# The last image's gate taken from sums of numerators, its last product in two halves, its flag earlier, its last store on ScalarE

## The chip, the cores and the metric

One core of a Trainium2 chip runs the kernel. The metric is the device time of one execution in microseconds; the kernel before has a median of 2622.44 us over three runs. Engines are named as the profile names them: PE is TensorE (PEld its weight loads), DVE is VectorE, ACT is ScalarE, POOL is GpSimd, SP is SyncE; a q behind a name is the engine's sequencer. Times without a unit's origin count from the start of the profiled span.

## What is computed

A batch of 16 images of 256 channels, 28 x 28, passes through a residual block whose two convolutions are lookups: each channel's 3 x 3 patch is softly assigned to 16 centroids, and the assignment weights mix a table.

```python
def amm_conv3x3(x, centroids, w_sub, stride=1):
    patches = jax.lax.conv_general_dilated_patches(x, (3, 3), (stride, stride), 'SAME')
    ...
    d = jnp.sum(p * p, axis=-1)[..., None] - 2.0 * jnp.einsum('bncs,cks->bnck', p, centroids) + ...
    attn = jax.nn.softmax(-d, axis=-1)
    lut = jnp.einsum('cks,cso->cko', centroids, w_sub)
    out = jnp.einsum('bnck,cko->bno', attn, lut)
def se_layer(x, w1, b1, w2, b2):
    s = jnp.mean(x, axis=(2, 3))
    s = jax.nn.relu(s @ w1 + b1)
    s = jax.nn.sigmoid(s @ w2 + b2)
    return x * s[:, :, None, None]
out = amm_conv3x3(x, centroids1, wsub1); out = jax.nn.relu(bn_inference(out, ...))
out = amm_conv3x3(out, centroids2, wsub2); out = bn_inference(out, ...)
out = se_layer(out, se_w1, se_b1, se_w2, se_b2)
return jax.nn.relu(out + x)          # x here: group-normed; the block's input is added once more outside
```

What matters here is the end: the gate `s` of an image needs the mean of all 784 positions of the second convolution, after its batch norm, before a single output value can be written.

## The kernel before

Per layer and image there are four blocks: two halves of the input channels times two halves of the 28 rows (392 positions, `N`). A block makes logits (line 418), exponentials, numerators (`na`, `nb`, lines 469 and 483) and a reciprocal, and ends with nine scaled numerator tiles `q` of 128 x 392 (`qp` in pairs of 784 columns, `qo` single). Eight products a image and layer then combine the `q` of four blocks with weights by Strassen's scheme (Winograd's form): seven multiplications of 128-channel halves, numbered 5 to 12 after their place in the schedule (6 and 7 are one, cut in two). A product is nine matmuls of 128 x 128 by 128 x 392, fp32, each of which leaves two records in the profile. POOL forms the differences of `q` in place (`mix`, lines 560 and 562); VectorE, ScalarE and POOL combine the products' results into four regions: c11, c12 (output half 0, row halves 0 and 1), c21, c22 (output half 1).

The order of work is written out by hand: `at(cl, sub, f, ...)` files a job under a place, all jobs are sorted by place and issued in that order, and each engine takes its own instructions in that order. For the last image of layer 2 (`n == 2 * B - 1`, b = 15), `g` is its first place, products 9 to 12 stand at `g + 9` to `g + 12`, and no later block fills TensorE. PSUM is four tiles of two banks each (`ps0` to `ps3`); a tile is given by a turning rule (`ROLES`, `EARLY`) or by a fixed `tag`, and a new user of a tile waits until the last reader of the old one is done.

End of an image in layer 2: batch norm with a running sum (`norm_out`, line 608, or `norm_both`, line 617), `se_hidden` (lines 839 to 851, a matmul over the means and two small activations), `se_gate` (853 to 862, a matmul and exponentials), `se_recip` (865), and the finish. For images 0 to 14 the finish is spread over ScalarE and POOL while later blocks run: `finish_gate` (869), `finish_norm` (877, group norm of x into `xn`), `finish_sum` (883), `finish_relu` (888), `finish_add` (891), `store` (902). For image 15 it is `finish_fast`: two VectorE passes a half, lines 896 and 899, and the store by SP. Product 12 enters c21 by line 592, which is the last thing that the mean waits for.

Numerator sums have a second use: `wsum` collects the sums of every block, and `flags` (lines 911 to 922) checks them for overflow; `flag_sum` (924) adds the flags over partitions with a matmul and casts the sum to an integer. Every engine loads that integer (line 1170), and where it is positive a slow fallback runs (line 1172 on); here it is skipped by a branch.

## Time and profile before

| | |
|---|---|
| median of 3 runs | 2622.44 us (2621.93 to 2623.15) |
| profiled execution | 2621.02 us |
| its span | 2619.5 us |
| PE busy | 2583.4 us (99%) |
| DVE, ACT, POOL busy | 1761.6, 1360.3, 1900.5 us |
| granted TensorE clock, mean | 0.998 |

The span is one execution as the hardware profiler saw it; the time of a run has some 1.5 us more around it. A timeline row gives start, duration, engine, line, operation, tiles and, in brackets, the idle time before it and who ended it. A matmul's recorded duration is longer than its share of a stream, since matmuls overlap: a product's pace is read from starts or from the chain of waits. ACTIVATION_READ_ACCUMULATOR rows belong to the activation with a running sum before them.

### The profile page before, as it was taken

Reading aid. Unit: us, or ns where it says so; the run is one execution under the profiler, and the core shown is the slowest. Engines: PE = TensorE matmul, PEld = TensorE weight load, DVE = VectorE, ACT = ScalarE, POOL = GpSimd, SP = SyncE. Lnnn points to the kernel's source line nnn. Section 1 sums busy time; section 2 is a strip of 40 time slices with the busy share of each in tenths; the row PEclk is TensorE's granted clock in tenths of the full one; section 3 lists DMA queues with packets and bytes.
Section 4 is the critical chain, followed back from the end, with each engine's and each line's share of the span. In section 5 each row is a group of like instructions: output and inputs, shape, how many; then the busy total and the mean of one; then the engine's idle time right before and its main releaser. Section 6 shows DMA issues by size and latency. Waiting matters only on the chain.

```text
span 2619.5 us, 85666 instructions
## 1 busy us (share of the span) xinstructions
PE 2583.4 (99%) x36984; PEld 1265.0 (48%) x36984; DVE 1761.6 (67%) x3759; ACT 1360.3 (52%) x1879; POOL 1900.5 (73%) x1316
## 2 busy tenths in 40 slices
PE   6999999999999999999999999999999999999997
PEld 2444454444444444444444444444444444444444
DVE  5776656666566665566676767766776767677665
ACT  5444544444444454444445555555555556555553
POOL 3786666766568766677666887878878778878786
PEclk9999999999999999999999999999999999999999
DMA  8556656655555566554664444444444443444441
GB/s 223 157 162 180 196 152 188 169 170 173 155 144 148 168 184 178 166 166 135 179 168 103 112 109 129 119 122 119 103 118 128 126 117 104 117 123 121 117 121 45
DMA packets 217959, 374.37 MB, mean 143 GB/s; under 512 B 29752, under 2 KB 188520, under 8 KB 217576
## 3 DMA queue, kind: packets, MB, share of 16 engines
q1 hardware_dynamic: 211256, 335.24, 48.1%
q0 software_dynamic: 6320, 33.58, 3.6%
q8 instruction: 295, 4.83, 0.8%
q14 instruction: 88, 0.72, 0.1%
HBM read 288.93 MB, written 79.80 MB: 141 GB/s over the span
## 4 chain that ended last, share of the span: by engine, by line
PE 97%; DMA 1%; DVE 1%; POOL 0%; ACT 0%; SPq 0%; issue 0%; DVEq 0%; POOLq 0%; ACTq 0%
PE acc L553 52%; PE lg L418 17%; PE na L469 14%; PE nb L483 14%; DMA wall<-home 0%; DMA pt<-home 0%; PE sep L855 0%; DVE r L511 0%; SPq L404 0%; ACT e L429 0%; POOL qp L562 0%; PE sep L844 0%; DMA home<-xpad 0%; DMA xt<-in_x 0%; DVE rb L526 0%
## 5 line engine op out<-in xcount | busy, mean ns | idle before, releaser
L553 PE MATMUL acc<-qp,wall 128*128 128x392 f32 x3072 | 1096.8, 500 | 0.9 <-DVE qp L545 0.7
L429 ACT ACTIVATE e<-lg 128x784 f32<-128x784 f32 x960 | 737.9, 820 | 635.1 <-PE lg L418 632.2
L562 POOL TENSOR_TENSOR qp<-qp,qp 128x784 f32<-128x784 f32 x512 | 943.5, 1867 | 155.6 <-DVE qp L545 155.1
L553 PEld LDWEIGHTS acc<-qp,wall 128*128 128x128 f32 x3072 | 566.4, 190 | 507.1 <-issue 56.9
L526 DVE STREAM_SHUFFLE rb<-r 128x392 f32<-128x392 f32 x1024 | 551.0, 604 | 0.0
L418 PE MATMUL lg<-pt,wd 32*32 32x392 f32 x16256 | 483.2, 502 | 7.2 <-DMA wall<-home 4.9
L497 DVE SCALAR_TENSOR_TENSOR r<-nb,kst,r 128x392 f32<-128x392 f32 x128 | 80.1, 626 | 458.6 <-ACT r L493 444.1
L545 DVE TENSOR_TENSOR qp<-na,rb 128x784 f32<-128x784 f32 x352 | 333.8, 972 | 59.4 <-PE na L469 48.2
L483 PE MATMUL nb<-e,cwb 64*32 64x392 f32 x8192 | 373.6, 492 | 0.1
L469 PE MATMUL na<-e,cwa 64*32 64x392 f32 x8192 | 373.7, 492 | 0.0
L534 POOL TENSOR_TENSOR qo<-qo,rb 128x392 f32<-128x392 f32 x128 | 132.5, 1035 | 310.2 <-DVE rb L522 309.4
L511 DVE RECIPROCAL r<-r 128x392 f32<-128x392 f32 x128 | 333.2, 2603 | 4.4
L534 POOL TENSOR_TENSOR qp<-qp,rb 128x784 f32<-128x784 f32 x160 | 295.8, 1858 | 3.2 <-ACT hpad L604 0.4
L483 PEld LDWEIGHTS nb<-e,cwb 64*32 64x32 f32 x8192 | 189.5, 107 | 176.6 <-issue 20.8
L469 PEld LDWEIGHTS na<-e,cwa 64*32 64x32 f32 x8192 | 182.2, 106 | 182.4 <-issue 72.9
L418 PEld LDWEIGHTS lg<-pt,wd 32*32 32x32 f32 x16256 | 120.9, 103 | 281.8 <-issue 243.1
L553 PE MATMUL acc<-qp,w_A 128*128 128x392 f32 x512 | 182.7, 499 | 0.0
L493 ACT ACTIVATE r<-nb,kst 128x392 f32<-128x392 f32 x128 | 86.7, 678 | 162.3 <-PE nb L483 162.3
L453 POOL TENSOR_TENSOR z<-z,mx 128x1568 f32<-128x1568 f32 x32 | 91.8, 2869 | 94.8 <-DVE mx L447 94.8
L553 PE MATMUL acc<-qo,wall 128*128 128x392 f32 x384 | 157.8, 493 | 0.0
L539 ACT COPY qp<-na 128x784 f32<-128x784 f32 x160 | 130.0, 812 | 26.2 <-PE na L469 24.4
L553 PEld LDWEIGHTS acc<-qp,w_A 128*128 128x128 f32 x512 | 94.7, 190 | 82.1 <-DVE qp L545 19.8
(159 smaller groups left out, 1642.8 us busy)
## 6 DMA issues: line engine op xcount, KB each, us to landing
pt<-home SPq DMA_DIRECT2D x762, 209.0 KB
pt<-home SPq DMA_DIRECT2D x762, 104.5 KB
home<-xpad SPq DMA_DIRECT2D x30, 899.0 KB
xt<-in_x SPq DMA_DIRECT2D x30, 784.0 KB
out_dram<-y SPq DMA_DIRECT2D x32, 392.0 KB
d_wS<-st SPq DMA_DIRECT2D x12, 192.0 KB
wall<-d_wS SPq DMA_DIRECT2D x4, 576.0 KB
wall<-in_ws SPq DMA_DIRECT2D x3, 576.0 KB
```

The source lines that it names most:

```text
L418: nc.tensor.matmul(bk[32 * c : 32 * c + 32, :N].rearrange("p (r w) -> p r w", w=W), lhsT=wts["wd", u["hh"]][32 * i : 32 * i + 32, mm, c, : ...
L429: nc.scalar.activation(eg[:, 2 * i : 2 * i + 2, :], bk[:, :, :N], AF.Exp, scale=2.0)
L453: nc.gpsimd.tensor_tensor(zk, zk, mx.unsqueeze(2).to_broadcast([P, N // 4, K]), ALU.subtract)
L469: nc.tensor.matmul(bs[32 * i : 32 * i + 32, r, :N], lhsT=wts["cwa", u["hh"]][64 * r : 64 * r + 64, mm, i, :], rhs=es[64 * r : 64 * r + 64, ...
L483: nc.tensor.matmul(bs[32 * i : 32 * i + 32, r, :N], lhsT=wts["cwb", u["hh"]][64 * r : 64 * r + 64, mm, i, :], rhs=es[64 * r : 64 * r + 64, ...
L511: nc.vector.reciprocal(u["r"], u["r"])
L526: nc.vector.stream_shuffle(rb[:, r, :], u["r"], mask_of(2 * mm + r))
L534: nc.gpsimd.tensor_tensor(q, q, u.pop(("rb", mm)), ALU.mult)
L539: nc.scalar.copy(pair(u, mm), u.pop(("na", mm))[:, :, :N])
L545: nc.vector.tensor_mul(pair(u, mm), u.pop(("na", mm))[:, :, :N], rb)
L553: nc.tensor.matmul(accs[key][:, :N], lhsT=wl[w][:, k, :], rhs=us["q", k], start=first and n == 0, stop=last and n == len(ks) - 1,)
L562: nc.gpsimd.tensor_tensor(pair(out_u, mm), pair(in0, mm), pair(in1, mm), ALU.subtract)
```

## The change

- **Sums instead of products for the gate** (image 15). The mean of product 11's and product 12's results over positions is the weight matrix times the sum of the `q` over positions. ScalarE sums each of the nine `q` of block 0 (`total_act`, an activation with running sum whose output is thrown away), VectorE those of block 3 (`total_dve`); POOL takes their difference, since product 12 uses block 0 minus block 3 (`total_sub`). ScalarE multiplies the nine 128 x 128 weight blocks of A12 and of A22 by these sums, one activation a block (`weigh`), VectorE adds the nine (`weigh_sum`), and two one-column matmuls against ones add over partitions (`rest_sum`). `norm_ahead` norms c11 and c21 before those products are in, with their running sums; `se_hidden` adds the two missing means as further terms.
- **Product 11** is issued in three parts (5, 2 and 2 matmuls): rest_sum's matmuls stand between the first two, se_hidden and the flag's matmul between the last two, and se_gate's matmul before product 12. **Product 12** is issued as two halves of 196 columns in PSUM tiles 2 and 3 (`open_last`). Its result is no longer added to c21 and normed; `finish_ahead` folds gate, norm and x for the 392 positions beforehand, and `finish_last` takes each half from PSUM with two passes of 196 columns. c11, c12 and c22 are finished (`norm_join`, `finish_part`) ahead of them.
- **The flag**: `flags` moves behind rest_sum, `flag_sum` into product 11.
- **Stores**: image 15 has four instead of two: 784, 392 and 196 columns by SP, the last 196 by ScalarE.
- **Image 14** is finished by two activations into PSUM tile 3 (`gate_wide`) and two VectorE passes each (`finish_wide`) instead of by ScalarE and POOL; its norm of x moves ahead, to before product 9.
- **Image 15's x** is loaded into a patch buffer instead of an exponential's, at `g + 7` instead of `g + 11`, and normed at `g + 8`; products 9, 10 and 11 get PSUM tiles 0, 1 and 0. POOL's subtraction for the first pair at `g + 10` comes just before the others.

The diff, cut to its core:

```diff
+    def spare_of(n0, n, i=0):
+        return pts[i].rearrange("p s n -> p (s n)")[:, n0 : n0 + n]
...
+    def product(key, us, w, ks, first=True, last=True, step=None, cols=(0, N), tag=None):
+        if first and key not in accs:
+            accs[key] = bank("acc", step, step and ROLES["acc"][step % 2], EARLY["acc"].get(step) if tag is None else tag)
         for n, k in enumerate(ks):
             nc.tensor.matmul(
-                accs[key][:, :N], lhsT=wl[w][:, k, :], rhs=us["q", k],
+                accs[key][:, : cols[1] - cols[0]], lhsT=wl[w][:, k, :], rhs=us["q", k][:, cols[0] : cols[1]],
...
+        terms = [(k, ysum[:, k, i : i + 1]) for k in range(NB) for i in range(2 if b >= B - 1 else 1)]
+        if (b, "rest") in ys:
+            terms += [(k, ys[b, "rest"][:, k : k + 1]) for k in range(NB)]
+        for n, (k, term) in enumerate(terms):
+            nc.tensor.matmul(ps, lhsT=w1_sb[:, k, :], rhs=term, start=n == 0, stop=n == len(terms) - 1)
...
+    def gate_wide(b, k):
+        ys[b, "g"] = banks("gp", tag=3)[:, :, :N]
+        y = ys[b, k].rearrange("p (t n) -> p t n", t=2)
+        nc.scalar.activation(ys[b, "g"], y, AF.Copy, scale=se[b][:, k : k + 1])
+
+    def finish_wide(b, k):
+        y, g = (t.rearrange("p (t n) -> p t n", t=2) for t in (ys[b, k], ys[b, "t"][:, HW * k : HW * k + HW]))
+        ps = ys.pop((b, "g"))
+        nc.vector.tensor_tensor(ps, ps, g, ALU.add)
+        nc.vector.scalar_tensor_tensor(
+            y, ps, 0.0, xs[b][:, k].rearrange("p (t n) -> p t n", t=2), op0=ALU.max, op1=ALU.add
+        )
...
+    def total_dve(u, mm):
+        if mm == 4:
+            nc.vector.tensor_reduce(qsum[:, 0, 8:9], u["q", 8], axis=AX.X, op=ALU.add)
+        else:
+            nc.vector.tensor_reduce(qsum[:, 0, 2 * mm : 2 * mm + 2], pair(u, mm), axis=AX.X, op=ALU.add)
+
+    def total_act(u, k):
+        nc.scalar.activation(
+            spare_of(NB * S * P, N, 1), u["q", k], AF.Identity, bias=zero, scale=one, accum_out=qsum[:, 1, k : k + 1]
+        )
+
+    def total_sub():
+        nc.gpsimd.tensor_tensor(qsum[:, 1], qsum[:, 1], qsum[:, 0], ALU.subtract)
...
+    def weigh(o, ks):
+        for k in ks:
+            nc.scalar.activation(
+                spare_of(o * S * P, S * P, 1).rearrange("p (n k) -> p n k", k=S)[:, :, k], wl["A22" if o else "A12"][:, k, :], AF.Copy, scale=qsum[:, o, k : k + 1]
+            )
+
+    def weigh_sum(o):
+        v = spare_of(o * S * P, S * P, 1).rearrange("p (n k) -> p n k", k=S)
+        nc.vector.tensor_reduce(vsum[:, o, :], v, axis=AX.X, op=ALU.add)
+
+    def rest_sum(b, tag):
+        ps = bank("pv", tag=tag)[:, :NB]
+        for o in range(NB):
+            nc.tensor.matmul(ps[:, o : o + 1], lhsT=vsum[:, o, :], rhs=one, start=True, stop=True)
+        ys[b, "rest"] = rest[:, 1]
+        nc.vector.tensor_tensor(rest[:, 1], ps, rest[:, 0], ALU.mult)
...
+    def norm_ahead(b, o, dst=None):
+        sc, sh = bn[1]
+        src = region(1, b, o, 0)
+        nc.scalar.activation(
+            src if dst is None else dst, src, AF.Identity, bias=sh[:, o : o + 1], scale=sc[:, o : o + 1],
+            accum_out=sum_of(b, o, 0),
+        )
...
+    def norm_join(b, key):
+        nc.vector.scalar_tensor_tensor(
+            region(1, b, 0, 0), accs.pop(key)[:, :N], bn[1][0][:, 0:1], ahead(), op0=ALU.mult, op1=ALU.add
+        )
...
+    def finish_part(b, k, n0, n1):
+        y, x0 = ys[b, k][:, n0:n1], xs[b][:, k, n0:n1]
+        t = ys[b, "t"][:, HW * k + n0 : HW * k + n1]
+        nc.vector.scalar_tensor_tensor(y, y, se[b][:, k : k + 1], t, op0=ALU.mult, op1=ALU.add)
+        nc.vector.scalar_tensor_tensor(y, y, 0.0, x0, op0=ALU.max, op1=ALU.add)
+
+    def finish_ahead(b):
+        t = ys[b, "t"][:, HW : HW + N]
+        nc.vector.tensor_tensor(rest[:, 2, 1:2], se[b][:, 1:2], rest[:, 0, 1:2], ALU.mult)
+        nc.vector.scalar_tensor_tensor(t, ys[b, 1][:, :N], se[b][:, 1:2], t, op0=ALU.mult, op1=ALU.add)
+
+    def finish_last(b, key, n0, n1):
+        y, x0 = ys[b, 1][:, n0:n1], xs[b][:, 1, n0:n1]
+        t = ys[b, "t"][:, HW + n0 : HW + n1]
+        nc.vector.scalar_tensor_tensor(
+            y, accs.pop(key)[:, : n1 - n0], rest[:, 2, 1:2], t, op0=ALU.mult, op1=ALU.add
+        )
+        nc.vector.scalar_tensor_tensor(y, y, 0.0, x0, op0=ALU.max, op1=ALU.add)
+
+    def store_part(b, k, n0, n1):
+        eng = nc.scalar if n0 == N // 2 else nc.sync
+        eng.dma_start(out[b, k * P : (k + 1) * P, n0:n1], ys[b, k][:, n0:n1])
...
+    def open_last(n):
+        accs[n, 12], accs[n, 13] = bank("acc", tag=2), bank("acc", tag=3)
...
+                elif n == 2 * B - 1 and c == 11:
+                    for sub, k0, k1 in ((1.95, 0, 5), (1.97, 5, 7), (1.99, 7, 9)):
+                        at(g + c, sub, product, (n, c), us[r], w, ks[k0:k1], k0 == 0, k1 == 9, tag=0)
+                elif n == 2 * B - 1 and c in (9, 10):
+                    at(g + c, 2.0, product, (n, c), us[r], w, ks, tag=c - 9)
+                elif n == 2 * B - 1 and c == 12:
+                    at(g + c, 1.99, open_last, n)
+                    for h in range(2):
+                        at(g + c, 2.0 + 0.02 * h, product, (n, 12 + h), us[r], w, ks, cols=(N // 2 * h, N // 2 * h + N // 2))
...
+            if n == 2 * B - 1:
+                at(g + 8, 1.92, turn_sign)
+                at(g + 8, 1.93, norm_ahead, b, 0, ahead())
+                for k in KO:
+                    at(g + 9, 1.5, total_act, us[0], k)
+                for mm in (1, 2, 3, 4):
+                    at(g + 9, 1.5, total_dve, us[3], mm)
+                at(g + 10, 0.02, total_dve, us[3], 0)
+                at(g + 10, 0.5, weigh, 0, KO)
+                at(g + 10, 0.52, weigh_sum, 0)
+                at(g + 10, 1.405, total_sub)
+                at(g + 10, 1.5, weigh, 1, KO)
+                at(g + 10, 1.51, norm_ahead, b, 1)
+                at(g + 11, 1.8, weigh_sum, 1)
                 at(g + 11, 1.9, norm_out, l, b, *c12)
                 at(g + 11, 1.91, norm_out, l, b, *c22)
-                at(g + 12, 1.9 if l else 0.05, norm_out, l, b, *c11)
+                at(g + 11, 1.96, rest_sum, b, 1)
+                at(g + 11, 1.98, se_hidden, b, None, 1)
+                at(g + 11, 1.995, se_gate, b, None, 1)
+                at(g + 12, 0.0, norm_join, b, (n, 11))
+                at(g + 12, 0.01, se_recip, b)
+                at(g + 12, 0.02, finish_part, b, 0, 0, HW)
+                at(g + 12, 0.02, store_part, b, 0, 0, HW)
+                at(g + 12, 0.03, finish_part, b, 1, N, HW)
+                at(g + 12, 0.03, store_part, b, 1, N, HW)
+                at(g + 12, 0.04, finish_ahead, b)
+                for h in range(2):
+                    at(g + 12, 2.01 + 0.02 * h, finish_last, b, (n, 12 + h), N // 2 * h, N // 2 * h + N // 2)
+                    at(g + 12, 2.01 + 0.02 * h, store_part, b, 1, N // 2 * h, N // 2 * h + N // 2)
+            else:
+                at(g + 12, 0.0, acc_add, l, b, c11, (n, 11))
+                at(g + 12, 2.02, acc_add, l, b, c21, (n, 12), op=ALU.subtract)
...
+                near = b == B - 2
+                at(*((g + 7, 0.6) if last else (g + 13, 2.6)), load_x, b, last)
                 for q in range(NB):
-                    at(*((g + 12, 0.4) if last else (g + 19, 1.9)), finish_norm, b, q)
-                    if not last:
+                    at(*((g + 8, 1.9) if last else (g + (16 if near else 19), 1.9)), finish_norm, b, q)
+                if not last:
+                    at(g + 14, 2.1, se_hidden, b, g + 14)
+                    at(g + 17, 2.1, se_gate, b, g + 17, 2 if near else None)
+                    at(g + 18, 0.3, se_recip, b)
+                    for q in range(NB):
+                        if near:
+                            at(*((g + 19, 1.95) if q else (g + 18, 0.35)), gate_wide, b, q)
+                            at(*((g + 19, 1.965) if q else (g + 18, 0.36)), finish_wide, b, q)
+                            at(*((g + 19, 1.965) if q else (g + 18, 0.36)), store, b, q)
+                            continue
...
-                    else:
-                        at(g + 14, 1.92, finish_fast, b, q)
-                        at(g + 14, 1.92, store, b, q)
                 if b == B - 1:
-                    at(g + 11, 1.9, flags)
-                    at(g + 12, 2.9, flag_sum)
+                    at(g + 11, 1.962, flags)
+                    at(g + 11, 1.985, flag_sum)
```

More of the change, by code (lines that the diff above doesn't have):

```diff
@@ L297, with small_bank @@
     cst = const.tile([P, 64], F32, name="cst")
-    def small_bank(name, step):
-        return bank(name, step, step and ROLES["small"][step % 2], EARLY["small"].get(step))
+    def small_bank(name, step, tag=None):
+        return bank(name, step, step and ROLES["small"][step % 2], EARLY["small"].get(step) if tag is None else tag)
     def center_sq(wf, c0, w, eng=None):
@@ L547 @@
     accs = {}
-    def product(key, us, w, ks, first=True, last=True, step=None):
-        if first:
-            accs[key] = bank("acc", step, step and ROLES["acc"][step % 2], EARLY["acc"].get(step))
+    def product(key, us, w, ks, first=True, last=True, step=None, cols=(0, N), tag=None):
+        if first and key not in accs:
+            accs[key] = bank("acc", step, step and ROLES["acc"][step % 2], EARLY["acc"].get(step) if tag is None else tag)
         for n, k in enumerate(ks):
             nc.tensor.matmul(
-                accs[key][:, :N], lhsT=wl[w][:, k, :], rhs=us["q", k],
+                accs[key][:, : cols[1] - cols[0]], lhsT=wl[w][:, k, :], rhs=us["q", k][:, cols[0] : cols[1]],
                 start=first and n == 0, stop=last and n == len(ks) - 1,
@@ L837, with se_hidden @@
     se = {}
-    def se_hidden(b, step=None):
+    def se_hidden(b, step=None, tag=None):
         ysum = ys[b, "sum"]
-        ps = small_bank("sep", step)[: 2 * RED, :1]
-        terms = [(k, i) for k in range(NB) for i in range(2 if b >= B - 1 else 1)]
-        for k, i in terms:
-            nc.tensor.matmul(
-                ps, lhsT=w1_sb[:, k, :], rhs=ysum[:, k, i : i + 1],
-                start=(k, i) == terms[0], stop=(k, i) == terms[-1],
-            )
+        ps = small_bank("sep", step, tag)[: 2 * RED, :1]
+        terms = [(k, ysum[:, k, i : i + 1]) for k in range(NB) for i in range(2 if b >= B - 1 else 1)]
[3 more added lines that the diff above has]
+            nc.tensor.matmul(ps, lhsT=w1_sb[:, k, :], rhs=term, start=n == 0, stop=n == len(terms) - 1)
         hid = small.tile([2 * RED, 1], F32, name="se_hid")
@@ L851, in se_hidden, with se_gate @@
         nc.scalar.activation(se[b], halves, AF.Copy, scale=hid)
-    def se_gate(b, step=None):
-        ps = small_bank("sep", step)[:, :NB]
+    def se_gate(b, step=None, tag=None):
+        ps = small_bank("sep", step, tag)[:, :NB]
         nc.tensor.matmul(ps, lhsT=w2_sb, rhs=se[b], start=True, stop=True)
```

37 lines of the change are left out of this document (25 added, 12 removed).

## The prediction

> **What bounds the kernel now.** The page first: its span and its fourth part, the shares of the chain that ended last. Then, for the last 35 us alone, the chain of waits in order of time.
>
> ```profile
> span 2619.5 us, 85666 instructions
> ...
> PE 97%; DMA 1%; DVE 1%; POOL 0%; ACT 0%; SPq 0%; issue 0%; DVEq 0%; POOLq 0%; ACTq 0%
> ```
> ```profile
> 2587.67 17.98 PE acc L553 x54
> ...
> 2605.74 0.57 DVE y L592
> ...
> 2607.20 0.30 PE sep L844 x4
> ...
> 2609.34 0.18 DVE se_gt L865
> ...
> 2609.55 1.05 DVE y L896
> ...
> 2612.57 0.98 DVE y L899
> ```
>
> TensorE sets the time until 2605.65 us. All that the change touches lies in what follows: the serial tail of the last image, in which TensorE computes only scraps. Products 10, 11 and 12 are 54 records in 17.98 us, 0.333 us each and 5.99 us a product, so product 11 runs from 2593.66 to 2599.66. From 2605.65 to the end of the last VectorE instruction (2613.55) pass 7.90 us: 3.9 for add, norm, hidden layer and gate up to the start of L896, 4.0 for four passes over 784 columns. The last 5.95 us are store and program end; for these I read the rows of the lines of the store, the flag's load and the branch behind it.
>
> ```profile
> L902 SPq DMA_DIRECT2D out_dram<-y x4: 332/344/357, 2603.8 to 2613.6; - x4
> ...
> L1170 ACTq TENSOR_LOAD <-fi x1: 465/465/465, 2609.0 to 2609.0; - x1
> ...
> L1172 SPq EVENT_SEMAPHORE  x8: 17/17/17, 2617.3 to 2617.9; - x8
> ...
> L1172 ACTq COMPARE_BRANCH  x1: 50/50/50, 2609.5 to 2609.5; - x1
> L1172 ACTq EVENT_SEMAPHORE  x1: 17/17/17, 2612.1 to 2612.1; - x1
> ...
> L1172 SPq COMPARE_BRANCH  x1: 45/45/45, 2614.6 to 2614.6; - x1
> ...
> L1322 SPq DRAIN  x3: 7/7/13, 2618.7 to 2619.0; - x3
> ```
>
> SP issues the last store at 2613.6, loads the flag, branches at 2614.6 and is back at 2617.3. Its eight waits, the store's landing among them, pass in 0.6 us, so the landing is hidden behind the branch's 2.7 us. The rest of SP's list takes until 2618.7, and the closing barrier 0.8.
>
> **The change, part by part.** *The gate from numerators.* The last image's mean no longer waits for products 11 and 12: ScalarE and VectorE sum the numerators, weigh 18 weight blocks by the sums, and two one-column products give the missing means. Whether the work is hidden is decided engine by engine.
>
> ```profile
> 2572.55 0.68 ACT L503 ACTIVATE qo<-nb,kst 128x392 f32<-128x392 f32 x1 [0.70 <-DVE r L497]
> 2579.38 0.81 ACT L539 COPY qp<-na 128x784 f32<-128x784 f32 x1 [6.16 <-PE na L469]
> 2587.70 0.41 ACT L858 ACTIVATE se_gt<-sep,nb_sb 128x1 f32<-128x1 f32 x2 [7.51 <-PE sep L855]
> 2588.15 0.29 ACT L861 ACTIVATE se_gt<-se_gt,one 128x2 f32<-128x2 f32 x1
> 2588.68 1.79 ACT L869 ACTIVATE y<-y,se_gt 128x784 f32<-128x784 f32 x2 [0.23 <-DVE se_gt L865]
> ...
> 2594.48 0.71 ACT L608 ACTIVATE y<-y,bnsh,bnsc 128x392 f32<-128x392 f32 x1 [2.16 <-DVE y L590]
> 2595.10 0.19 ACT L608 ACTIVATION_READ_ACCUMULATOR y<-y,bnsh,bnsc 128x1 f32 x1
> 2595.20 0.70 ACT L608 ACTIVATE y<-y,bnsh,bnsc 128x392 f32<-128x392 f32 x1
> ```
> ```profile
> L447 DVE TENSOR_REDUCE mx<-z 128x98 f32<-128x1568 f32 x32 | 56.8, 1776 | 0.0
> ```
>
> ScalarE's 6.16 us hole takes four norms of x (about 1.0 each; half of L869's pair is 0.90), two small scalings (0.2) and norm_ahead (0.72, the step between the two L608): 5.1, hidden. The 7.51 us hole takes nine total_act at 0.72: 6.5, ready about 2586.7, hidden. VectorE's five total_dve cost 0.89 a pair (1.776 x 784/1568) in holes of its own; the last ends about 2589.3 and delays the reciprocal of image 14's gate by 0.9, to 2589.5. Then ScalarE: gate_wide 0.90 to 2590.45, and 18 weigh of 128 columns. None is in the trace; between 0.205 (one column, half of L858's pair) and 0.72 (392 columns), so 3.7 to 13 us; by the line from one column to 784, 0.32 each: 5.7, to 2596.2. weigh_sum is 1152 columns, 1.30: to 2597.5. TensorE has done ten records of product 11 at 2597.0, so it waits 0.5 us there; the two one-column products and rest_sum end near 2598.0.
>
> *The early flag.* flags now follows rest_sum on VectorE, and the flag's matmul stands inside product 11, ahead of its last four records.
>
> ```profile
> 2593.88 0.57 DVE L590 TENSOR_TENSOR y<-acc,y 128x392 f32<-128x392 f32 x1 [5.24 <-PE acc L553]
> 2594.37 1.28 DVE L914 TENSOR_SCALAR ok<-wsum 128x128 f32<-128x128 f32 x1
> ...
> 2597.18 1.19 DVE L918 TENSOR_SCALAR csum<-csum 128x2 f32<-128x2 f32 x1
> ...
> 2598.60 0.15 DVE L920 TENSOR_SCALAR fl<-fl 128x1 f32<-128x1 f32 x1
> 2598.79 1.38 DVE L921 TENSOR_TENSOR fl<-fl 128x1 f32<-128x1 f32 x1
> ```
> ```profile
> 2595.53 1.01 POOL L560 TENSOR_TENSOR qo<-qo,qo 128x392 f32<-128x392 f32 x1
> 2596.51 1.84 POOL L562 TENSOR_TENSOR qp<-qp,qp 128x784 f32<-128x784 f32 x1
> 2598.32 3.65 POOL L883 TENSOR_TENSOR y<-y,xn 128x784 f32<-128x784 f32 x2
> ```
>
> Ahead of them VectorE stood idle for 5.24 us (the first row): room for the first finish_wide of image 14 (1.95, from 2590.5) and for weigh_sum's first call. The nine flag instructions took 5.8 us, though L920 on one column takes 0.15. Each long one ends where POOL passes from one instruction to the next: L914 at 2595.65 (2595.53), L918 at 2598.37 (2598.32), L921 at 2600.17 (the middle of L883's pair, 2600.15). The change takes L883 and L891 off POOL for this image pair, so POOL falls silent at 2598.35 plus total_sub (some 0.2). I therefore take the first flag instruction to end at 2598.7 and the others at their short steps, 0.19 each and 0.45 for the reduction: flags end near 2600.3. Bounds: 1.7 us from 2598.0 (2599.7) and the old 5.8 (2603.8). TensorE reaches the flag's matmul near 2599.5 and stands 0.8 us; behind this wait, as behind that for weigh_sum, stand the last records of product 11, the gate's product and all of product 12.
>
> The Trainium skill, "SBUF — State Buffer", section "Who interferes with whom", has VectorE and GpSimd share one port pair under an exclusive lock, taken also by a VectorE instruction with two SBUF inputs, and the loser blocks fully. The trace agrees: L921, two inputs of one column, took 1.38 us. By that rule alone the five flag instructions after POOL's end would be short, which is the value taken.
>
> *Two tiles.* Product 12's halves take banks 2 and 3. Bank 3 is freed by finish_wide of image 14, bank 2 by the cast of the flag, which stands behind it on VectorE.
>
> ```profile
> L545 DVE TENSOR_TENSOR qp<-na,rb 128x784 f32<-128x784 f32 x352 | 333.8, 972 | 59.4 <-PE na L469 48.2 <-issue 6.6
> ...
> L508 DVE SCALAR_TENSOR_TENSOR qo<-nb,kst,qo 128x392 f32<-128x392 f32 x128 | 67.6, 528 | 0.0
> ```
> ```profile
> L855 PEld LDWEIGHTS sep<-se_hh,w_sb 32*128 32x128 f32 x4 | 0.6, 183 | 1.3 <-ACT se_hh L851 0.8 <-issue 0.6
> ```
>
> After the flags VectorE does finish_wide (0.97 + 0.98) and the cast (0.14): 2602.4. TensorE itself, after four records (1.33) and the gate product (0.3), would be ready at 2602.2. Product 12 starts near 2602.55 instead of 2599.66: **2.9 us lost**. The halves are 36 records of 196 columns: 0.167 each if the loads hide. Two loads of 128 columns take 0.29 together and 0.183 singly, so one every 0.11, under 0.167: hidden, 6.1 us with the start, to 2608.65. If a load added to each record, 9.9; but the 392-column records show no such addition, so I take the low end.
>
> Under this cover VectorE does norm_join (0.57), reciprocal, one finish_part of 784 columns (1.05 + 0.98), one of 392 (0.57 + 0.53) and finish_ahead (0.7): from 2602.4 to about 2607.3 with the gate's wait; then the first half's two instructions, to 2607.9. Cover left: 0.8 us; without it the same time falls on the end. The second half: two passes of 196 columns, 0.31 each (0.98 less 1.5 times the step from 0.98 to 0.53): VectorE ends at 2608.65 + 0.1 + 0.65 = **2609.4 against 2613.55: 4.15 us won**.
>
> *Last store by ScalarE.* SP is free after the first half's store at 2607.9, branches, is back near 2611.5 and has only ScalarE's landing to wait for; that store is a quarter of the old bytes. ScalarE: issue 0.33 (SP's; ScalarE issues none in this trace: 0.1 to 1.3, four of SP's), load 0.47, branch to wait 2.6 (2609.5 to 2612.1), about 3.6 with the steps between: ready at 2613.05, then the barrier's 0.8. The end lies 4.5 us behind VectorE instead of 5.95: **1.4 us won**. The two stores moved ahead of it and the x load moved from product 11's time to about 2557 lie on SP with nothing waiting behind them.
>
> Sum: 2619.5 - 4.15 - 1.4 = 2613.95, less 5.5 us. The profiled execution took 2621.02 with 1.5 us outside the span, 1.4 below the median of 2622.44; I put the difference on the median: **2616.9**. What the measurement can tell from no change is 0.2%, 5.2 us, so the forecast stands almost on that line.
>
> **Rivals.** *A stalls more, gain kept under 5.2 us.* weigh at 0.5 each puts the one-column products at 2601, flags at 2602.7 and product 12 at 2605: gain 3, 2619.4. ScalarE's first store at 1.3 costs 1 us: 2617.9. For it: 18 unmeasured instructions and two queues in series; against: the flag's wait absorbs the first 0.8 us.
>
> *B hardly stalls, gain larger.* If the sums are ready at 2597 and flags take 1.7 without POOL, product 12 starts near 2600.9, and the end is 1.6 earlier: 2615.3. For it: L920's 0.15; against: finish_wide still stands before the cast, and VectorE's 4.9 us of cover work then nearly sets the end itself.
>
> *C slower.* TensorE stands so long that its clock falls.
>
> ```profile
> 2608.00:2610.00 2.00, 0.38 (x2) 0.29 (x2) 0.62 (x2) 0.81 (x4) 0.00 (x0) 0.86 0.04 12
> 2610.00:2612.00 2.00, 0.00 (x0) 0.00 (x0) 1.97 (x3) 0.00 (x0) 0.00 (x0) 0.50 0.01 4
> ```
>
> The granted clock (third from the right) went from 1 to 0.5 near 2609.4 (0.86 = mean over 2 us), 3.8 us after the last product, with scraps between. If flags took their old 5.8 us, TensorE would wait for the flag from 2599.5 to 2603.8, 4.3 us: over that point. Product 12 would start at 2605.9 at half clock, 12.2 us, and the end come at 2605.9 + 12.2 + 0.75 + 4.5 = 2623.4, 3.9 later: 2626.3. It decides from 3.8 us of standing; I expect 0.8. The Trainium skill, "TensorE: Matmul & The Clock Gate", section "What's actually happening", gives an idle window of about 3.4 us before the clock halves; the trace's 3.8 agrees.
>
> *D the change doesn't shorten the chain*, as the gate comes behind product 12 after all: the gate's product stands before product 12 in TensorE's order, so I give it nothing.
>
> **How the numbers follow.** The forecast's own terms, each at its nearer bounds (flags ready 0.6 earlier to 0.7 later, ScalarE's issue 0.2 less to 0.5 more, its way through the branch 2.6 to SP's 2.7 and 0.3 more), reach from 2615.9 to 2618.3; some six tenths of that lie below 2617.2, the line of 0.2%. Chances: forecast 0.48, of which 0.29 below that line; B and gains between it and the forecast 0.33, since it asks only that 18 short instructions and nine shorter ones run at the pace of the shortest row; A 0.12; C 0.07. Faster by over 0.2%: 0.29 + 0.33 = 0.62. Within: 0.19 + 0.12 = 0.31. Slower by over 0.2%: 0.07. Range 2614.3 to 2620.3: it reaches a microsecond below B and past A, and leaves out C and the ends of the others.
>
> **What would show it.** TensorE's waits in product 11: under 1 us before the one-column products and about 0.8 before the flag's matmul; product 12 starting 2.9 us later than now; flags in some 2.3 us, none ending at a POOL boundary after 2598.6; 36 records at 0.167; VectorE idle before the second half; 4.5 us from VectorE's last end to the span's. Wrong if a record of 196 columns takes over 0.2, if the granted clock falls inside product 12, or if ScalarE's store takes over 1 us to issue.

## The result and the profile after

| | before | changed |
|---|---|---|
| median of 14 runs each | 2623.37 us (2621.12 to 2626.83) | 2617.11 us (2615.36 to 2621.54) |
| ratio, 95% interval | | 0.9977 (0.997 to 0.9984) |
| profiled execution / its span | 2621.02 / 2619.5 us | 2617.13 / 2615.7 us |
| start of the last block's reciprocal to VectorE's last end | 41.00 us | 36.00 us |
| the same start to the span's end | 46.95 us | 40.81 us |

The change made the kernel faster: 6.26 us between the medians, hardly more than the 0.2% that the prediction took as its line. The last two rows use a fixed point, the start of the last long RECIPROCAL on VectorE (2572.55 before, 2574.89 after); what the change touches lies almost all behind it. Distances from it are compared throughout, since the two profiled executions don't reach it at the same time (last section). The changed kernel's page has the same shares as before, so it doesn't help here; the chain of waits of its last 36 us does. Columns: start, time on the chain, engine, tile, line, records.

```profile
...
2582.89 6.12 PE acc L555 x18
2589.01 0.31 PE sep L856 x2
2589.32 9.41 PE acc L555 x28
2598.74 0.51 PE pv L953 x4
...
2599.42 0.87 DVE ok L1014
...
2601.78 0.19 PE flp L1026 x2
...
2603.83 6.22 PE acc L555 x36
...
2610.08 0.43 DVE y L992
...
2610.53 0.36 DVE y L995
```

Before, the chain left TensorE at 2605.65 and ran 7.9 us over VectorE and ScalarE, with scraps of TensorE between them. Now it leaves TensorE only for the flag (2599.26 to 2601.74) and for the last 0.8 us. The view that sums TensorE's waits from 2571 us on shows which are left, the changed kernel's first, then the kernel's before:

```profile
PE flp L1026 <- DVE fl L1022: 0.7, 1, 0.7
PE acc L555 <- POOL qp L564: 0.2, 1, 0.2
```
```profile
PE sep L844 <- DVE fi L927: 0.7, 1, 0.7
PE sep L855 <- ACT se_hh L851: 0.7, 1, 0.7
PE acc L553 <- DVE qp L545: 0.7, 1, 0.7
...
```

The third row of before is no part of the tail: it is product 9, which waited 0.65 us for its PSUM tile. It is gone, because the change gives products 9 to 11 fixed tiles (shown by e4 below).

VectorE's and POOL's timelines of the changed kernel (start, duration, then the row) show the sums and the flag:

```profile
2597.44 1.35 DVE L948 TENSOR_REDUCE pt<-pt 128x128 f32<-128x1152 f32 x1 [0.80 <-ACT pt L942]
...
2599.34 0.95 DVE L1014 TENSOR_SCALAR ok<-wsum 128x128 f32<-128x128 f32 x1
2600.21 0.21 DVE L1015 TENSOR_SCALAR ok<-wsum 128x128 f32<-128x128 f32 x1
...
2603.55 0.14 DVE L1027 CAST fi<-flp 1x1 int32<-1x1 f32 x1
...
2604.60 0.17 DVE L866 RECIPROCAL se_gt<-se_gt 128x2 f32<-128x2 f32 x1 [0.39 <-ACT se_gt L862]
...
2610.08 0.42 DVE L992 SCALAR_TENSOR_TENSOR y<-acc,rest,pt 128x196 f32<-128x196 f32 x1 [0.56 <-PE acc L555]
```
```profile
2598.35 1.86 POOL L564 TENSOR_TENSOR qp<-qp,qp 128x784 f32<-128x784 f32 x1
```

weigh_sum ends at 2598.79. The one-column products stand on the chain from 2598.74, the one that needs weigh_sum being the second of them, and the list of waits has none for them. L1014 takes 0.95 us and ends at 2600.29, just behind POOL's last mix (2600.21); the other flag instructions are short. In the cover under product 12 VectorE still has 0.39 + 0.56 us of idle time.

The way out of the program, by the rows of the branch and the closing drain (count, shortest/median/longest in ns, first and last start):

```profile
L1320 SPq EVENT_SEMAPHORE  x8: 17/17/17, 2613.3 to 2613.8; - x8
...
L1320 SPq COMPARE_BRANCH  x1: 45/45/45, 2610.5 to 2610.5; - x1
L1320 DVEq COMPARE_BRANCH  x1: 76/76/76, 2611.2 to 2611.2; - x1
...
L1320 ACTq COMPARE_BRANCH  x1: 54/54/54, 2611.9 to 2611.9; - x1
L1320 ACTq EVENT_SEMAPHORE  x1: 17/17/17, 2612.4 to 2612.4; - x1
L1320 DVEq EVENT_SEMAPHORE  x1: 21/21/21, 2614.6 to 2614.6; - x1
```
```profile
L1470 POOLq DRAIN  x3: 46/103/6607, 2607.0 to 2615.4; - x3
L1470 SPq DRAIN  x3: 7/7/13, 2614.8 to 2615.1; - x3
```

From branch to the first event behind it SP takes 2.8 us, VectorE 3.4 and ScalarE 0.5. So SP and VectorE end last, not ScalarE with its store.

### The profile page after: what moved, and what is told of

It reads as the page before. It is cut to its first block, busy times and chain, and to the rows that moved or that the text cites. A ratio compares the mean times of both kernels' runs of the same rounds, so it can differ in the third digit from the quotient of the medians.

```text
span 2615.7 us, 85783 instructions
## 1 busy us (share of the span) xinstructions
PE 2587.5 (99%) x37010; PEld 1267.0 (48%) x37010; DVE 1769.8 (68%) x3776; ACT 1370.8 (52%) x1915; POOL 1893.6 (72%) x1313
## 4 chain that ended last, share of the span: by engine, by line
PE 97%; DVE 1%; DMA 1%; POOL 0%; SPq 0%; ACT 0%; issue 0%; POOLq 0%
PE acc L555 52%; PE lg L420 17%; PE nb L485 14%; PE na L471 14%; DMA pt<-home 0%; SPq L406 0%; DVE r L513 0%; PE sep L856 0%; POOL qp L564 0%; DMA home<-xpad 0%; DMA xt<-in_x 0%; PE sep L848 0%; DVE gn_st L342 0%; DVE rb L528 0%; PE gnp L348 0%
## 5 line engine op out<-in xcount | busy, mean ns | idle before, releaser
L555 PE MATMUL acc<-qp,wall 128*128 128x392 f32 (+1 forms) x3088 | 1097.7, 498 | 0.3 <-POOL qp L564 0.2
L555 PE MATMUL acc<-qo,wall 128*128 128x392 f32 (+1 forms) x386 | 157.9, 491 | 0.0
```

What stands on the lines that cost most here:

```text
L555: nc.tensor.matmul(accs[key][:, : cols[1] - cols[0]], lhsT=wl[w][:, k, :], rhs=us["q", k][:, cols[0] : cols[1]], start=first and n == 0, s ...
```

## The experiments

Each is one edit of the changed kernel. "End" is the distance from the reciprocal's start to the span's end (40.8), "work" the one to VectorE's last end (36.00). e1 to e8 were timed once each, so their distances are compared and not their times.

**How far distances repeat** (e11_again: the changed kernel once more).

> The changed kernel itself, profiled once more: how far do the distances from the reciprocal's start repeat? VectorE's last instruction ends 36.0 us behind it in the first profile, the span's end 40.8. Theory (the work repeats to 0.1 us, the way back from the branches on SP and VectorE scatters, from 2.6 to 3.4 us in the runs so far): 35.9 to 36.1, and 40.5 to 41.4. Rival (the work itself scatters): 36.0 missed by more than 0.3.

Work 36.02, end 40.48. In this one repetition the work comes back to 0.02 us, and the way out differs by 0.3. Small differences are therefore read from the work, and an end is trusted to some 0.4 us. The median of 10 runs was 2619.0 us beside 2623.33 before, ratio 0.998 (0.997 to 0.999).

**The store back on SP** (e1_sp_store).

```diff
-        eng = nc.scalar if n0 == N // 2 else nc.sync
-        eng.dma_start(...)
+        nc.sync.dma_start(...)
```

> Only the last store goes back from ScalarE to SP. I measure each profile from the start of the last block's reciprocal on VectorE (128x392) to the end of the span: 46.95 us before, 40.81 with the change. Theory: what the ScalarE store buys is that SP's load of the flag, branch and return (0.55 + 0.05 + 2.75 us) no longer follow the last store: 41.9 here, 1.1 longer. Rival, by the Trainium skill, SKILL page 'Trainium Kernel Development and Optimization', section 'Key Constraints' (issuing from several engines only saves the sequencer's issue time): 0.3 to 0.4 longer, 41.2. Second rival: VectorE's own return from the branch (3.4 us after its last instruction in the changed kernel's profile) sets the end either way: no difference.

Work 35.99, end 42.01: 1.2 to 1.5 us later than the two profiles of the changed kernel. SP now issues the store 36.0 us behind the reciprocal's start instead of its previous one at 34.7, and its load, its branch and the way back start that much later. The store's new queue is worth what it takes SP out of the line, as predicted (1.4). The expectation of 41.9 held; the two rivals (41.2, and no difference) did not.

**The flag late** (e2_late_flag: its matmul and cast behind product 12 again).

```diff
-        ps = bank("flp", tag=2)[:, :1]
+        ps = bank("flp", tag=1)[:, :1]
...
-                    at(g + 11, 1.985, flag_sum)
+                    at(g + 12, 2.9, flag_sum)
```

> Only the flag's matmul and cast go back behind product 12 (the flag's terms stay where they are, the flag's PSUM tile becomes number 1). Theory A, of the prediction: the flag's place matters by TensorE's wait for it (0.7 us) and by the cast ahead of product 12; behind product 12 product 12 starts 0.7 earlier and the end moves by under 1 us either way: 40 to 41.8 from the last block's reciprocal to the end. Theory B, from comparing the two profiles: GpSimd needs a fixed time from the cast to its last drain's end (10.4 us before, 2606.4 to 2616.7; 10.0 with the change, 2603.6 to 2613.6); with the cast near the end of the second half that sets the end: about 4 to 6 us longer, 45 to 47.

The work, counted here to the last pass (the cast follows it by 0.06 us), is 35.08, 0.9 earlier than in the changed kernel, since TensorE stands nowhere for the flag; the end is 45.89, 5.1 later, as theory B had it. The rows of POOL in this run say why:

```profile
L1320 POOLq COMPARE_BRANCH  x1: 45/45/45, 2609.7 to 2609.7; - x1
...
L1320 POOLq INC_SWDGE_SEM  x1: 1792/1792/1792, 2610.6 to 2610.6; - x1
```
```profile
L1470 POOLq DRAIN  x3: 46/103/6607, 2612.5 to 2619.6; - x3
```

POOL needs the flag to leave; behind its branch come 1.8 us of a semaphore step and a drain of 6.6 us, from 2612.5 to 2619.1. From the cast's end at 2609.14 to the end of this drain are 9.9 us, and the closing barrier comes behind it. The same drain stands in the changed kernel from 2607.0 to 2613.6, also 9.9 us behind the cast's end, and is harmless by 1.1 us beside SP's 2614.8. So the early flag isn't a trifle: with the flag's matmul and cast behind product 12, all the rest of the change gains 1.1 us at the end instead of 6.1.

**Product 12 whole** (e3_whole12: one tile, one pair of passes of 392 columns).

```diff
-        accs[n, 12], accs[n, 13] = bank("acc", tag=2), bank("acc", tag=3)
+        accs[n, 12] = bank("acc", tag=2)
...
-                        at(g + c, 2.0 + 0.02 * h, product, (n, 12 + h), us[r], w, ks, cols=(N // 2 * h, N // 2 * h + N // 2))
+                    at(g + c, 2.0, product, (n, 12), us[r], w, ks)
...
```

> Only the halves are undone: product 12 is one run of 18 records of 392 columns in PSUM tile 2, finished in two VectorE passes of 392 and stored at once by ScalarE. Theory: TensorE's time is the same (36 records of 0.166 against 18 of 0.329), and only the last two passes are longer, 0.57 + 0.55 against 0.42 + 0.36: 0.35 to 0.6 us longer, 41.2 to 41.4 from the last block's reciprocal to the end. Rival: the halves cost as much as they save (VectorE does four passes for two): no difference, 40.8.

Work 36.36, end 41.24, as expected. The halves are worth 0.36 us. The first of the two passes that stand behind product 12 starts at the same distance (35.13 here, 35.19 in the changed kernel), and both are longer: 0.62 and 0.57 instead of 0.42 and 0.36.

**Tiles 9 and 10 by the turning rule** (e4_role_tiles).

```diff
-                elif n == 2 * B - 1 and c in (9, 10):
-                    at(g + c, 2.0, product, (n, c), us[r], w, ks, tag=c - 9)
```

> Products 9 and 10 of the last image get their PSUM tiles by the turning rule again instead of the fixed tiles 0 and 1; all else as in the change. Theory: product 9's old tile is one that the last block's numerators still occupy, so TensorE waits 0.65 us for VectorE's third multiplication (the wait in the profile of before, gone in the changed kernel's): 0.65 longer if it passes through to the end, 41.4 from the last block's reciprocal to the end; 40.9 if later waits swallow it (TensorE's wait for the flag, 0.7). Rival: the wait went away by the other order of subtractions on GpSimd or by chance: no wait before product 9 here either.

Work 38.03, end 42.68, more than any of the three expected values: the expected wait came, and two more with it. The waits of TensorE in this run:

```profile
PE sep L856 <- DVE y L592: 1.1, 1, 1.1
PE acc L555 <- DVE y L592: 0.7, 1, 0.7
PE acc L555 <- DVE qp L547: 0.7, 1, 0.7
```

The last row is product 9's old wait, 0.66. The first two are new: image 14's gate and product 11 meet tiles that VectorE's additions still hold. 1.13 + 0.73 + 0.66, less the flag's 0.66 that TensorE no longer stands, is 1.86 of the 2.03 us. The two lines that look like bookkeeping carry about a third of the gain.

**One more reduction in the flag's chain** (e6_one_more) **and four more** (e7_four_more).

```diff
+        for _ in range(1):     # e7: range(4)
+            nc.vector.tensor_reduce(fl[:, 2:3], spare_of(S * P, S * P, 1), axis=AX.X, op=ALU.max)
         nc.vector.tensor_reduce(fl[:, 2:3], csum, axis=AX.X, op=ALU.max)
```

> One more reduction of 1152 columns (1.35 us by L948) inside the flag's chain; its result is overwritten. TensorE's last record ahead of its wait ends at about 2600.6 in the changed kernel's time, so it stands 2.5 us instead of 1.1, the scraps of the gate's products among them. Theory that the wait passes on one for one and the clock holds: 40.8 + 1.35 = 42.1 us, granted clock 1.00 throughout. Rival that the cover on VectorE takes some of it: under 41.6. Rival C of the prediction (clock falls): not yet, as 2.5 is under 3.8 us; if the clock falls below 0.9 here, the bound of 3.8 us was wrong.

> Four more reductions of 1152 columns inside the flag's chain: TensorE stands 1.1 + 5.4 = 6.5 us, over the 3.8 us after which its granted clock fell in the kernel before. Rival C of the prediction: the clock falls to 0.5 before the flag's product, and the four records of product 11, the gate's product and all or part of product 12 run at half rate: 46.2 us plus 4 to 8 us: 50 to 54 us, 36 records of product 12 at up to 0.33. Theory that only the wait itself counts: 40.8 + 5.4 = 46.2 us and 0.167 a record.

With one more, the wait for the flag rose from 0.66 to 1.90 and the work from 36.00 to 37.28, one for one, the clock at 1.00 throughout. The end is 41.7 beside the expected 42.1, a difference that an end's scatter covers. With four more, TensorE's timeline and the granted clock (third column from the right of the windows):

```profile
2606.92 0.19 PE L1028 MATMUL flp<-fl 128*1 128x1 f32 x2 [6.06 <-DVE fl L1024]
2607.04 2.98 PE L555 MATMUL acc<-qp,wall 128*128 128x392 f32 x4
```
```profile
2605.00:2605.20 0.20, 0.00 (x0) 0.00 (x0) 0.20 (x1) 0.00 (x0) 0.00 (x0) 0.69 0.00 0
2611.80:2612.00 0.20, 0.20 (x3) 0.20 (x2) 0.20 (x1) 0.00 (x0) 0.00 (x0) 0.74 0.00 0
```

The work is 43.65, 7.65 later: 5.40 of longer standing and 2.2 of half clock. The end, 48.7, lies behind that of before (46.95). Rival C is real. Its price per lost clock was too high: the clock came back at 2611.90, 5 us after the work did, so only the rest of product 11 and part of product 12's first half ran slowly (four records took 2.98 instead of 1.58 us).

**The flags ahead of weigh_sum** (e5_flags_ahead).

```diff
-                    at(g + 11, 1.962, flags)
+                    at(g + 11, 1.79, flags)
```

> The nine flag instructions stand ahead of weigh_sum's second call instead of behind rest_sum, so GpSimd's last mixes run beside them. Measured from the start of the last block's reciprocal on VectorE to the span's end: 40.8 us in the changed kernel. Theory (VectorE's long flag instructions end only where GpSimd passes from one instruction to the next, as L1014 did at 2600.29): they start when the fourth addition L592 ends and two or three of them take 0.9 to 1.9 us, the chain 3 to 4 us instead of 1.6; weigh_sum starts when GpSimd's last mix ends, TensorE stands 2.5 to 3 us ahead of the one-column products L953 instead of being just in time, the wait of 0.66 for the flag is gone: 42.6 to 43.1 us. Rival (the length belongs to the first instruction of the chain or to its data, GpSimd doesn't matter): L1014 0.95, the rest short, TensorE stands 1.3 us: 41.3 to 41.5 us.

End 47.7: the theory missed it by 4.6 us, the rival by 6.2. First VectorE's long rows, then POOL's:

```profile
2594.67 0.96 DVE L1014 TENSOR_SCALAR ok<-wsum 128x128 f32<-128x128 f32 x1
2595.55 1.05 DVE L1015 TENSOR_SCALAR ok<-wsum 128x128 f32<-128x128 f32 x1
...
2597.16 1.18 DVE L1018 TENSOR_SCALAR csum<-csum 128x2 f32<-128x2 f32 x1
```
```profile
2591.87 3.68 POOL L564 TENSOR_TENSOR qp<-qp,qp 128x784 f32<-128x784 f32 x2
2595.49 1.03 POOL L562 TENSOR_TENSOR qo<-qo,qo 128x392 f32<-128x392 f32 x1
2596.47 1.85 POOL L564 TENSOR_TENSOR qp<-qp,qp 128x784 f32<-128x784 f32 x1
```

The theory of the flags held: three instructions took 0.96 to 1.18 us and ended at 2595.63, 2596.60 and 2598.34, each at a change on POOL (2595.55, 2596.52, 2598.32); two columns took 1.18 us, as before. The run with the turning rule (e4) gives the other side: there POOL was done at 2601.44, the flags began at 2602.62, and L1014 took 0.22 us. So it isn't the first instruction as such that is long. The chain took 4.2 us up to weigh_sum. TensorE stood 3.28 us at its second one-column product, near the 3 expected. What neither theory had was the clock:

```profile
2600.24 0.59 PE L953 MATMUL pv<-one,pt 128*128 128x1 f32 x2 [3.28 <-DVE pt L948]
2600.69 1.66 PE L555 MATMUL acc<-qp,wall 128*128 128x392 f32 x2
```
```profile
2599.80:2600.00 0.20, 0.00 (x0) 0.00 (x0) 0.20 (x1) 0.00 (x0) 0.00 (x0) 0.70 0.00 0
2610.00:2610.20 0.20, 0.20 (x3) 0.20 (x2) 0.20 (x1) 0.00 (x0) 0.00 (x0) 0.70 0.11 41
```

It fell at 2599.88, some 3 us after the last full record, and stayed at half until 2610.12. A stand of 3.28 us cost 7.0 us of work: 2.6 by itself, since the 0.66 for the flag fell away, and 4.4 by the clock.

**The gate behind product 12** (e8_gate_behind: hidden layer, gate product and everything that uses the gate filed behind product 12; the sums stay).

```diff
-                at(g + 11, 1.98, se_hidden, b, None, 1)
-                at(g + 11, 1.995, se_gate, b, None, 1)
...
-                at(g + 12, 0.01, se_recip, b)
...
+                at(g + 12, 2.05, se_hidden, b, None, 1)
+                at(g + 12, 2.055, se_gate, b, None, 1)
...
+                at(g + 12, 2.06, se_recip, b)
...
```

> The gate still comes from the numerators, but its hidden layer and its product stand behind product 12 on TensorE, and all that uses the gate behind that. Theory (the gain of the changed kernel is the cover that product 12 gives to gate and finish): product 12 ends as before at about 33.2 us behind the reciprocal's start... then hidden layer, gate and reciprocal 2.4 us and 5.4 us of passes on VectorE: 40.8 + 7.0 = 47.8 us, more than the 47.0 of the kernel before. Rival D of the prediction (the place of the gate doesn't matter, the store and the tiles made the gain): 40.8 to 42 us.

Work 43.13, 7.13 later, end 48.58. VectorE's row shows the cover that was lost:

```profile
2612.11 0.17 DVE L866 RECIPROCAL se_gt<-se_gt 128x2 f32<-128x2 f32 x1 [8.12 <-ACT se_gt L862]
```

The gate's place carries the gain: with the gate behind product 12 this kernel ends later than the one before (46.95). That the gate comes behind product 12 after all, as the prediction's rival D had it, the changed kernel's own row rules out: its L866 starts at 2604.60, product 12 ends near 2610.05.

**A version that doesn't wait for the flag** (e9_flag_behind11), **and that cuts product 12 at 256 columns too** (e10_both, once more as e12_both_again).

```diff
-                    at(g + 11, 1.985, flag_sum)
+                    at(g + 11, 1.993, flag_sum)      # the matmul alone
+                    at(g + 11, 1.9931, flag_cast)
...
-                            at(*((g + 19, 1.965) if q else (g + 18, 0.36)), finish_wide, b, q)
+                            at(*((g + 19, 1.965) if q else (g + 18, 0.36)), finish_wide, b, q, 0)
+                            at(*((g + 19, 1.994) if q else (g + 18, 0.361)), finish_wide, b, q, 1)
...
+    CUT = (0, 256, N)     # the second version: instead of (0, 196, N)
```

> The flag's product moves behind the last four records of product 11, and the cast of the flag between the two passes of finish_wide, so that neither TensorE nor the first half's tile waits for the flag. From the reciprocal's start to the span's end 40.8 us in the changed kernel. Theory (the wait of 0.66 us at the flag is on the path, and VectorE's own idle time of 0.39 + 0.56 us in the cover absorbs the shift): product 12 starts 0.65 us earlier, 40.1 to 40.25 us. Rival (VectorE's cover sets the end: it can't start earlier than finish_wide ends): 40.6 to 40.9 us.

> As the run before, and product 12 cut at 256 columns instead of 196, so that two passes of 136 columns stand behind TensorE instead of two of 196. Theory (a record takes what its columns take, 0.116 us for 136): 0.15 to 0.2 us more, 39.9 to 40.1 us. Rival (a record can't be shorter than its weight load lets it; the 196-column records already run at that limit): 18 records of 0.217 and 18 of 0.167 are 6.9 instead of 6.0 us, 40.9 to 41.1 us.

> The version with the flag behind product 11 and the cut at 256 columns, once more, beside the changed kernel on the same chip. VectorE's last instruction ended 35.14 us behind the reciprocal's start, the span 40.33. Theory: 35.0 to 35.3 again and an end 0 to 0.9 us earlier than the changed kernel's, since SP's way back or the last store's landing now ends last; the medians differ by less than their scatter lets one tell.

TensorE has no wait left but POOL's 0.2. The work is 35.28 with the flag moved and 35.14 and 35.13 with the cut as well: 0.72 and 0.87 us won, as the theories had it. The records of 136 columns aren't held up by their weight loads: product 12 takes 6.2 us from its start to the end of its last record with either cut. In the second version the wait of VectorE for the last half is gone, so its own passes now set the work's end:

```profile
2607.86 0.42 DVE L1000 SCALAR_TENSOR_TENSOR y<-y,pt 128x256 f32<-128x256 f32 x1
2608.32 0.36 DVE L997 SCALAR_TENSOR_TENSOR y<-acc,rest,pt 128x136 f32<-128x136 f32 x1
```

The ends are another matter: 40.84 in the first, inside the rival's range but not by the rival's cause, for the work did come earlier; here SP took 3.3 us from its branch instead of the 2.8 and 2.5 of the changed kernel's profiles, and 40.33 and 40.21 in the second. Of 0.87 us of work some 0.4 arrive at the end (40.27 beside 40.64, means of two), which is no more than an end is trusted to. Medians of 10 runs each on one chip: 2617.56 us (ratio to before 0.9978, 0.9969 to 0.9988) beside the changed kernel's 2619.0 (0.998, 0.997 to 0.999). On another chip, where the changed kernel was not timed, the two versions had 2617.07 and 2615.71 us, 0.9969 and 0.9967 of before. The cut version is at least as good; that it is faster, the times alone don't show.

## Why the prediction was right, step by step

The predicted time, 2616.9, is 0.2 from the median. That it is so near is luck: two errors of 0.8 and 0.9 us with opposite signs nearly cancel. The gain was larger than the 5.5 us of the sum (6.26 between the medians, 6.1 and 6.5 by the two profiles), and the median of the kernel before came out 0.9 above the 2622.44 from which the sum was taken.

- **The sums are hidden**: right, with terms that cancel. A total_act step takes 0.84 to 0.90 us and not 0.72, so the nine end at 2590.2, 1.2 us later behind the reciprocal's start than predicted; but 18 weigh take 5.48 us instead of 5.7, and counted from product 11's first record (2595.37 in the chain, 9.41 x 18/28 behind 2589.32) weigh_sum ends 3.4 us later instead of the predicted 3.8. TensorE's predicted 0.5 us there is nothing.
- **The flag**: right. First instruction held until POOL's end, the rest short, 2.4 us in all (predicted 2.3); TensorE stands 0.66 (0.8). The run with the flags ahead shows the hold for three instructions. The rule of the Trainium skill, "SBUF — State Buffer", section "Who interferes with whom", that a VectorE instruction which takes the port pair shared with GpSimd waits until GpSimd's instruction is done, agrees with the held rows (L1014 in the changed kernel; L1014, L1015 and L1018 with the flags ahead). Not every instruction is held: beside them L1016 took 0.42 us and L1017 0.15 while POOL worked. That the port is the reason, no run here isolates.
- **Product 12**: it starts 8.5 us behind product 11's first record (8.9 predicted), 36 records take 6.22 (6.1), clock 1.00.
- **The end on VectorE**: passes of 196 columns take 0.42 and 0.36, not 0.31 each. From product 12's start to VectorE's end 7.06 us instead of 6.85. With the 0.4 above that makes 4.37 us won between products and VectorE's end, 4.15 predicted.
- **What was not in the sum**: 0.65 us of product 9, whose wait the diff removes by the tag in one line. The prediction went through the change from product 11 on and never looked at this wait. 4.37 + 0.65 = the 5.0 measured.
- **The store**: 1.2 to 1.5 us won (1.4); the end lies 4.5 to 4.8 us behind VectorE's (4.5), but by another way than the prediction put it. ScalarE issues in 0.38 us and is back from its branch in 0.5 instead of 2.6; SP with 2.8 and VectorE with 3.4 us end last. The step failed in its mechanism and held in its number. Why ScalarE came back in 2.6 us before and in 0.5 here stays open; its store isn't the reason, for with the store back on SP it took 0.5 us too.
- **Not seen**: POOL's 9.9 us from the flag to the end of its drain. The prediction took the early flag for a cost only (0.8 us of standing); it is what lets the rest of the gain reach the end.
- **Rivals A and B**: product 12 started 0.4 us earlier than forecast, counted from product 11; B asked for 1.65, A for later. Neither came.
- **Rival C**: the mechanism is real, "it decides from 3.8 us of standing" was wrong. 3.28 us sufficed in one run. Its price, product 12 wholly at half clock, was too high for 6 us of standing.
- **The range of the forecast's own terms**: a slip that changes nothing. The bounds as they are listed reach down to 2616.1, not 2615.9.

## What to carry to other kernels

When the last stretch of a kernel is shortened, list what each engine still has to do after its last input, drains and branches included: an engine with a fixed way out of 10 us, as POOL here, becomes the bound as soon as its last input comes less than 10 us before the others are done. In a diff, a tile that is given by hand instead of by a rule is an edit of its own, and its old wait is to be looked for. A stall of TensorE of 3 us or more, by the runs here, is priced with the clock that may fall, not with its length alone; stands up to 1.9 us left the clock at 1.00.

## What the runs showed of the hardware

- **The clock falls and rises on a raster.** Half clock lasted 10.24 us in one run (2599.88 to 2610.12), 6.82 in another (2605.08 to 2611.90), and 6.82 at the start of the changed kernel's profiled execution (28.78 to 35.60): three, two and two times 3.41. The stretch of full clock from the start to the fall at the end lasted 2577.06 us in eight of the 14 profiles, before and changed kernel among them, and 2580.48 in four: 755 and 756 times 3.4133. The fall came about 3 us after the last full record in the first and 4.7 in the second. The Trainium skill, "TensorE: Matmul & The Clock Gate", section "What's actually happening", states a free-running window of 3413 ns; the durations agree with it, and the delays fit a window whose phase differs from run to run. A window needn't be wholly idle for the clock to fall behind it: the one that ended with the fall at 2599.88, so from 2596.47 on, still held the end of product 11's records and the first one-column product, to 2596.97.
- **The same raster makes part of the scatter between runs.** In these three profiles TensorE's first blocks run at half clock until the raster lets it rise. The windows are from the changed kernel's start; the first pair of rows is the changed kernel's, the second that of before, and the last row is from the changed kernel's second profile.

```profile
28.00:29.00 1.00, 0.00 (x0) 0.00 (x0) 0.00 (x0) 0.00 (x0) 0.00 (x0) 0.89 0.52 117
35.00:36.00 1.00, 1.00 (x32) 0.36 (x23) 0.00 (x0) 0.00 (x0) 0.00 (x0) 0.70 0.55 117
```
```profile
29.63 3.30 PE L420 MATMUL lg<-pt,wd 32*32 32x392 f32 x64 [4.38 <-DMA pt<-home]
32.86 4.19 PE L485 MATMUL nb<-e,cwb 64*32 64x392 f32 x64
```
```profile
29.52 3.15 PE L418 MATMUL lg<-pt,wd 32*32 32x392 f32 x64 [4.92 <-DMA wall<-home]
32.60 2.87 PE L483 MATMUL nb<-e,cwb 64*32 64x392 f32 x64
```
```profile
32.52 3.96 PE L485 MATMUL nb<-e,cwb 64*32 64x392 f32 x64
```

  The clock rose at 35.60 us in the changed kernel's profile, at 32.39 before and at 34.80 in the second profile. In the last two these are the first clock records of the trace, and the windows view prints 1.00 for the time ahead of them; the pace says half, for 64 logit matmuls take 3.15 to 3.30 us there and 32 of them 0.94 us in the middle of the kernel. The second group took 4.19 us where the clock rose latest and 2.87 where it rose first, so of the 2.34 us by which the changed kernel's execution reached the reciprocal later, 1.3 are lost in that row alone. The second profile lost almost as much there (3.96) and yet started the reciprocal at 2573.82, 1.07 us before the first: the rest is not explained.
- **A way back from a taken branch differs by engine and run**: 2.5 to 3.4 us on SP, 2.9 to 3.6 on VectorE, and on ScalarE 2.6 before and 0.5 in every run of the changed kernel and its variants.
- **POOL's way out is long and nearly fixed.** From the end of the flag's cast to the end of its drain of 6.6 us pass 9.9 us in the changed kernel and with the late flag, and 10.4 before.
